# Five unread products per chunk in the gather loop of a graph-network kernel

## The chip, the cores and the metric

The kernel runs on one core of a Trainium2 chip. The metric is the device time of one execution in microseconds (us), as the median of several runs. The core has a tensor engine (PE), whose weight loads are listed apart as PEld, a vector engine (DVE), a scalar engine (ACT), GpSimd (POOL), a sync engine (SP) that issues transfers, and 16 DMA engines. The profile also lists the granted clock of the tensor engine as a share of full speed.

## The reference

The program is eight residual stages over a graph with 6250 nodes of 256 features and 100000 edges (`src`, `dst`): four graph layers and four mixtures of experts, in turn. Stage 3 is the second graph layer:

```python
def _L1_gnn_ref(vertex_features, edge_index, w0, w1):
    w0_features = vertex_features @ w0
    w1_features = vertex_features @ w1
    dst, src = (edge_index[0], edge_index[1])
    messages = w1_features[src]
    neighbours = jax.ops.segment_sum(messages, dst, num_segments=vertex_features.shape[0])
    return jax.nn.relu(w0_features + neighbours)
...
x = x + _L1_gnn_ref(_layernorm(x, axis=-1), edge_index, L1_gnn_w0, L1_gnn_w1)
```

It is called with `edge_index = jnp.stack([src, dst])`, so what the layer calls `dst` is the graph's `src`. Each node sums the transformed features of its neighbours.

## The kernel before

The stages run one after the other in one program, all unrolled. The features stay in on-chip memory as 49 tiles of 128 nodes (`X`), and each stage adds its result there.

Stage 3 has two halves. The first normalizes each tile, multiplies it by both weights, keeps the `w0` part in the accumulator `acc3` and writes the `w1` part to the table `w1d` in DRAM. A row of that table is 768 bf16 numbers: three bf16 parts of each of the 256 f32 values, so that their sum carries the precision of f32.

The second half is the loop of the change. The edges were sorted earlier, during stage 1, into buckets of 128 target nodes, and the buckets are cut into chunks of 256 edges (two lanes of 128). There are 448 chunks (`NCH`). Each chunk does this:

- On POOL, `gather` (line 631) fetches for each of the two lanes 128 rows of `w1d` by an indirect DMA into a tile `row3`. Six such tiles take turns (`s3g`, `bufs=6`), so a gather needs the tile of six gathers before, three chunks back.
- On DVE, once for every four chunks, line 1104 builds the one-hots `sel` of the target nodes of eight lanes. Two such tiles take turns.
- On PE, line 1113 forms six products of 256 columns: for each lane the one-hot matrix is the weight, and the three parts of the rows stream through. All six add up in one PSUM tile, `nbp` in the profile, of which there are two.
- On DVE, line 1116 adds this PSUM tile to the accumulator of the bucket, whose number DVE loads into a register, eight chunks at a time (`buckets`).

Beside the loop runs the sorting of stage 4's edges. It is a generator, `bucket_move`, of which `next(steps, None)` issues one step per chunk. It first counts edges per bucket (PE line 228, DVE line 220), then places them (PE lines 303 and 305, DVE's predicated copy on line 308), then moves them group by group (DVE's one-hots on lines 340 to 345, PE line 348) and scatters them to DRAM from POOL (line 327). Its products use PSUM tiles called `small` and `mv`.

The order on each engine in this stage is that of a list scheduler: an instruction that comes earlier in the program goes first when it is ready. The engines then work through their lists in order. Semaphores between them are placed from the tiles that instructions read and write.

Of the kernel before, what the change touches and what calls it, by code (L numbers as in the profile page):

```python
# [8 lines left out]
F = mybir.dt.float32  # L9
# [39 lines left out]
class Kern:  # L49
# [1013 lines left out]
    def stage3(self, S, routes):  # L1063

        tc, nc, A, X = self.tc, self.nc, self.A, self.X
        wd = self.dram.tile([NP, 3, D], BF, name="w1d")
        with ExitStack() as big:
            bp = big.enter_context(tc.tile_pool(name="s3", bufs=1))
            acc = bp.tile([128, NT, D], F, name="acc3")
            with ExitStack() as cx:  # L1070
                mp = cx.enter_context(tc.tile_pool(name="s3st", bufs=1))
                wp = cx.enter_context(tc.tile_pool(name="s3w", bufs=3))
                pp = cx.enter_context(tc.tile_pool(name="s3p", bufs=2, space=PSUM))
                W = self.kxm(mp, "W01", [A["L1_gnn_w0"], A["L1_gnn_w1"]])
                mv, rs = self.norm_stats(mp, wp, "s3")
                for t in range(NT):
                    hT = self.norm_T(wp, pp, mv, rs, t)
                    wps = pp.tile([128, 512], F, name="wps")
                    for k in range(2):
                        nc.tensor.matmul(wps, hT[:, k, :], W[:, k, :], start=(k == 0), stop=(k == 1))  # L1080
                    nc.scalar.activation(acc[:, t, :], wps[:, :D], AF.Copy)
                    o = wp.tile([128, 3, D], BF, name="w1o")
                    r = wp.tile([128, D], F, name="w1r")
                    self.parts([o[:, j] for j in range(3)], r, wps[:, D:])
                    nc.sync.dma_start(wd[t * 128:(t + 1) * 128], o)
            wdf = wd.rearrange("n j d -> n (j d)")
            with ExitStack() as cx:
                kp = cx.enter_context(tc.tile_pool(name="s3k", bufs=1))
                gp = cx.enter_context(tc.tile_pool(name="s3g", bufs=6))
                sp = cx.enter_context(tc.tile_pool(name="s3s", bufs=2))  # L1090
                pp = cx.enter_context(tc.tile_pool(name="s3q", bufs=2, space=PSUM))
                NCH, G = S["NCH"], 4
                iog = kp.tile([128, 128, 2 * G], BF, name="iog")
                nc.vector.tensor_copy(iog, self.iotab.unsqueeze(2).to_broadcast([128, 128, 2 * G]))
                locb = kp.tile([128, 2 * NCH], BF, name="locb3")
                nc.vector.tensor_copy(locb, S["sl"][:, :, 1])
                steps = routes(cx)
                for c in range(NCH):
                    next(steps, None)
                    b = self.buckets(S, c)  # L1100
                    if c % G == 0:
                        n = 2 * min(G, NCH - c)
                        sel = sp.tile([128, 128, 2 * G], BF, name="sel")
                        nc.vector.tensor_tensor(
                            sel[:, :, :n], iog[:, :, :n],
                            locb[:, 2 * c:2 * c + n].unsqueeze(1).to_broadcast([128, 128, n]),
                            ALU.is_equal)
                    ps = pp.tile([128, D], F, name="nbp")
                    for k in range(2):
                        row = gp.tile([128, 3 * D], BF, name="row3")  # L1110
                        self.gather(row, wdf, S["idx"][:, 2 * c + k, 0:1])
                        for j in range(3):
                            nc.tensor.matmul(ps, sel[:, :, 2 * (c % G) + k], row[:, j * D:(j + 1) * D],  # L1113
                                             start=(k + j == 0), stop=(k == 1 and j == 2))
                    ab = acc[:, ds(b, 1), :].rearrange("p o d -> p (o d)")
                    nc.vector.tensor_add(ab, ab, ps)
                for _ in steps:
                    pass
            for t in range(NT):
                nc.vector.scalar_tensor_tensor(X[:, t, :], acc[:, t, :], 0.0, X[:, t, :],  # L1120
                                               op0=ALU.max, op1=ALU.add)
# [1104 lines left out]
```

## Time and profile before

| what | value |
|---|---|
| median of 9 runs | 10914.83 us (10907.68 to 10940.94) |
| the profiled execution | 10896.95 us |
| its span, first to last instruction | 10895.2 us |
| instructions | 105592 |
| PE busy | 6449.9 us (59%), 32431 products |
| DVE busy | 5113.6 us (47%) |
| POOL busy | 4550.0 us (42%) |
| mean granted clock of PE | 0.729 |
| stage 3's loop | 3518.8 to 5045.0 us |

How to read it: a group of instructions is listed as line, engine, operation, the tile written and the tiles read, the number of instructions, then busy time in us and the mean of one in ns, and then the time that the engine sat idle just before them and what ended it. Products overlap in PE's pipeline, so the duration of one is longer than the distance from one start to the next. A list of waits gives who waited for whom, the us in total, the number of waits and the longest. A list of stretches gives start and end, the length, busy us and number of instructions of each engine, then the granted clock, the busy share of the DMA engines and GB/s.

### The profile page before, as it was taken

How to read it: one execution, taken by the hardware profiler on the slowest of the kernel's cores; microseconds unless marked ns; L12 is line 12 of the kernel's file. 1: busy time of each engine (PE TensorE's matmuls, PEld its weight loads, DVE VectorE, ACT ScalarE, POOL GpSimd, SP SyncE). 2: the span in 40 equal slices, each digit the busy share in tenths (PEclk: the TensorE clock that was granted, in tenths of full speed). 3: DMA queues.
4: the chain of work that ended last, by engine and by line, in shares of the span. 5: the costliest groups of instructions: out<-in, count | busy, mean ns of one | idle time of the engine just before them, and what ended most of it. 6: DMA issues, size and time to landing. Idle time of an engine off the chain costs nothing. (4 is left out here: it accounts for less than half of the span.)

```text
span 10895.2 us, 105592 instructions
## 1 busy us (share of the span) xinstructions
PE 6449.9 (59%) x32431; PEld 4201.3 (39%) x32431; DVE 5113.6 (47%) x13299; ACT 2222.3 (20%) x6799; POOL 4550.0 (42%) x4498
## 2 busy tenths in 40 slices
PE   4787657634794776665455555395555552742494
PEld 1345444422571333333233333174244442531363
DVE  5568755456314455543455555712333337333204
ACT  1243346520232000000222222131211110211120
POOL 0246655410123667673444444024266660243211
PEclk9888778765897766665566666597777775776597
DMA  3444356542662443334000000065444442452222
GB/s 130 149 137 112 108 149 195 157 119 79 193 209 92 136 125 106 104 107 91 7 7 7 7 7 7 2 214 167 115 122 117 121 114 75 153 155 47 54 78 66
DMA packets 613936, 1128.30 MB, mean 104 GB/s; under 512 B 156477, under 2 KB 420222, under 8 KB 599270
## 3 DMA queue, kind: packets, MB, share of 16 engines
q0 software_dynamic: 234752, 600.59, 21.0%
q1 hardware_dynamic: 320167, 454.29, 13.6%
q10 hardware_dynamic: 58412, 66.25, 2.0%
q8 instruction: 271, 4.44, 0.2%
q14 instruction: 334, 2.74, 0.1%
HBM read 930.96 MB, written 189.76 MB: 103 GB/s over the span
## 5 line engine op out<-in xcount | busy, mean ns | idle before, releaser
L766 PE MATMUL ops<-roww,ow 128*128 128x260 f32 (+1 forms) x3136 | 1017.5, 473 | 494.1 <-issue 288.7
L631 POOL DMA_INDIRECT roww<-kvd,saidx x784 | 845.8, 1079 | 1014.2 <-PE small L228 385.9
L631 POOL DMA_INDIRECT row<-gatd,scsl x864 | 817.0, 946 | 826.7 <-DVE pv L1684 542.3
L631 POOL DMA_INDIRECT row<-w1d,sbsl x896 | 901.7, 1006 | 551.9 <-issue 176.2
L631 POOL DMA_INDIRECT roww<-zd,saidx x784 | 813.5, 1038 | 581.8 <-issue 220.9
L766 PEld LDWEIGHTS ops<-roww,ow 128*128 128x128 f32 x3136 | 706.2, 239 | 702.4 <-issue 327.7
L1113 PE MATMUL nbp<-row,sel 128*128 128x256 bf16 x2688 | 566.0, 358 | 367.3 <-DMA row<-w1d,sbsl 216.2
L754 ACT ACTIVATE roww<-roww,pw 128x64 f32<-128x64 f32 x3136 | 756.9, 333 | 11.3 <-issue 9.2
L348 PE MATMUL mv<-orr,ol 128*128 128x234 f16 (+1 forms) x1824 | 545.3, 444 | 213.4 <-DVE orr L345 167.7
L1113 PEld LDWEIGHTS <-sel 128*128 128x128 bf16 x2688 | 366.0, 155 | 615.5 <-issue 335.3
L1030 PE MATMUL qe<-qw,ohT 128*128 128x256 bf16 x2352 | 419.4, 317 | 298.8 <-DVE roww L1033 229.8
L1649 DVE TENSOR_REDUCE mg<-P 128x4 f32<-128x1024 f32 x432 | 526.7, 1219 | 124.6 <-PE P L1644 83.1
L1352 PE MATMUL yp<-wr,hr 128*128 128x256 f32 x2176 | 537.9, 387 | 51.1 <-DVE yr L1355 50.8
L1390 PE MATMUL hp<-xr,wr 128*128 128x256 f32 x2176 | 535.8, 398 | 28.6 <-ACT hr L1392 19.0
L1355 DVE TENSOR_TENSOR yr<-yp,br 128x256 f32<-128x256 f32 x328 | 138.9, 424 | 861.7 <-PE yp L1352 806.6
L1149 PE MATMUL tps<-ident,xn 128*128 128x128 f32 x490 | 124.8, 404 | 686.0 <-DVE xn L126 470.1
L1641 PE MATMUL P<-identb,mb 128*128 128x512 bf16 x864 | 477.3, 552 | 11.9 <-issue 11.9
L1644 PE MATMUL P<-rb,sel 96*128 96x512 bf16 x864 | 466.2, 540 | 0.0
L1390 PEld LDWEIGHTS hp<-xr,wr 128*128 128x128 f32 x2176 | 401.7, 196 | 144.9 <-ACT hr L1392 29.2
L1033 DVE TENSOR_TENSOR roww<-roww,qe 128x512 f32<-128x512 f32 x448 | 270.6, 613 | 381.6 <-DMA roww<-kvd,saidx 199.1
L1352 PEld LDWEIGHTS yp<-wr,hr 128*128 128x128 f32 x2176 | 408.1, 194 | 106.8 <-DVE yr L1355 55.8
L1030 PEld LDWEIGHTS <-ohT 128*128 128x128 bf16 x2352 | 251.5, 112 | 442.9 <-issue 270.3
(629 smaller groups left out, 12520.5 us busy)
## 6 DMA issues: line engine op xcount, KB each, us to landing
wr<-in_moe_dram SPq DMA_DIRECT2D x108, 1026.0 KB
lr<-salaned SPq DMA_DIRECT2D x112, 448.0 KB
yd<-yr SPq DMA_DIRECT2D x164, 256.0 KB
wr<-in_moe_dram SPq DMA_DIRECT2D x56, 513.0 KB
eat<-in_edge_attr_dram ACTq DMA_DIRECT2D x32, 781.2 KB
qw<-qd SPq DMA_DIRECT2D x112, 192.0 KB
br<-in_L_ffn_b_dram SPq DMA_DIRECT2D x164, 128.0 KB
main<-osb SPq DMA_DIRECT2D x112, 129.0 KB
```

The lines of the kernel that those rows point to most:

```text
L348: nc.tensor.matmul(mv, ol[:, :, i], orr[:, 0:2, :, i], start=(c + i == c0), stop=(c + i == c0 + n - 1))
L631: return self.nc.gpsimd.indirect_dma_start(out=out, out_offset=None, in_=table, in_offset=bass.IndirectOffsetOnAxis(ap=idx, axis=0))
L754: nc.scalar.activation(x, x, AF.Copy, scale=p[:, j, i * H + h:i * H + h + 1])
L766: nc.tensor.matmul(ps[:, :VW], ow[:, j, :], row[:, j, v0:v0 + VW], start=(j == 0), stop=(j == BW - 1))
L1030: nc.tensor.matmul(ps[:, b], ohT[:, j + b, :], qw[:, k], start=(k == 0), stop=(k == 2))
L1033: nc.vector.tensor_mul(kr, kr, ps[:, :m])
L1113: nc.tensor.matmul(ps, sel[:, :, 2 * (c % G) + k], row[:, j * D:(j + 1) * D], start=(k + j == 0), stop=(k == 1 and j == 2))
L1352: nc.tensor.matmul(yp, hT[:, k, i * 128:(i + 1) * 128], w[:, O2 + k * D:O2 + (k + 1) * D], start=(k == 0), stop=(k == KH - 1))
L1390: nc.tensor.matmul(hp, w[:, k * H + m * 128:k * H + (m + 1) * 128], xe[:, k], start=(k == 0), stop=(k == 1))
L1641: nc.tensor.matmul(P[:, k], st["mb"][:, :, 2 * i + k], self.identb.unsqueeze(1).to_broadcast([128, 4, 128]), start=True, stop=False)
L1644: nc.tensor.matmul(P[:, k], sel[:, 2 * i + k, :], st["rb"], start=False, stop=True)
L1649: nc.vector.tensor_reduce(st["mg"][:, i, :], st["P%d" % i].rearrange("p k h e -> p h k e"), AX.XY, ALU.max)
```

## The change

Behind the six products of a chunk, five more are issued. Each multiplies the one-hots of the chunk's second lane with the first 512 columns of the second lane's row tile, and writes a PSUM tile `spare3` of 512 f32 columns, of which there is one. Each starts a sum of its own and ends it, and nothing reads the tile.

```diff
                 steps = routes(cx)
+                spare = pp.tile([128, 512], F, name="spare3", bufs=1)
                 for c in range(NCH):
...
                         for j in range(3):
                             nc.tensor.matmul(ps, sel[:, :, 2 * (c % G) + k], row[:, j * D:(j + 1) * D],
                                              start=(k + j == 0), stop=(k == 1 and j == 2))
+
+                    for _ in range(5):
+                        nc.tensor.matmul(spare, sel[:, :, 2 * (c % G) + 1], row[:, 0:512], start=True,
+                                         stop=True)
                     ab = acc[:, ds(b, 1), :].rearrange("p o d -> p (o d)")
                     nc.vector.tensor_add(ab, ab, ps)
```

## The prediction

> **What bounds the kernel now.** I read the page first, then the busy time of the engines in three parts of stage 3's loop, then the waits inside the loop, then TensorE's timeline, and last the loop in stretches of 20 us.
>
> The page says where the loop lies and who is busy in it: 448 chunks, 6 products each (2688) on line 1113, two gathers each (896) on line 631.
>
> ```profile
> L631 POOL DMA_INDIRECT row<-w1d,sbsl x896 | 901.7, 1006 | 551.9 <-issue 176.2
> L1113 PE MATMUL nbp<-row,sel 128*128 128x256 bf16 x2688 | 566.0, 358 | 367.3 <-DMA row<-w1d,sbsl 216.2
> ```
>
> The loop runs from the first gather at 3518.8 us to the last add at 5045.0, 1526 us. It has three parts: the first 480 us, in which other work counts and places stage 4's edges (512-column products of lines 228, 303, 305); 800 us of line 348's products with scatters; and a tail of 246 us with the loop alone. Busy time of PE, its granted clock, then DMA share and GB/s:
>
> ```profile
> 3520.00:4000.00 480.00, 357.69 (x1434) 0.72 0.49 138
> 4000.00:4800.00 800.00, 553.03 (x2290) 0.69 0.38 105
> 4800.00:5046.00 246.00, 119.34 (x463) 0.51 0.58 121
> ```
>
> PE is busy 1030 of 1526 us. POOL is the pacer: 896 gathers and 144 scatters are busy 1056 us, and 0.30 us of issue lies before each (1040 x 0.30 = 312), together 1368. The 158 us left are real waits; most name PE, since a gather has to wait until PE is done with the row of six gathers before:
>
> ```profile
> PE nbp L1113 <- DMA row<-w1d,sbsl: 216.2, 222, 10.2
> POOL row L631 <- PE nbp L1113: 140.9, 206, 4.6
> ```
>
> So the loop sits between two engines: PE waits for rows, and POOL for PE to free them. What PE is given more can lie in its 496 idle us, or come out as late rows.
>
> **What one added product costs.** Before has no product of these operands with 512 columns; the nearest are stage 4's bf16 products of 512, back to back (start, duration):
>
> ```profile
> 5399.90 0.63 PE L1644 MATMUL P<-rb,sel 96*128 96x512 bf16 x1
> 5400.33 0.63 PE L1641 MATMUL P<-identb,mb 128*128 128x512 bf16 x1
> ...
> 5404.13 0.38 PE L1641 MATMUL P<-identb,mb 128*128 128x512 bf16 x1
> 5404.35 0.38 PE L1644 MATMUL P<-rb,sel 96*128 96x512 bf16 x1
> ```
>
> The granted clock was 0.50 around the first pair and 1.00 around the second. From start to start that is 0.43 us at 0.50 and 0.22 at 1.00, so five cost 2.15 or 1.10 us per chunk, and 448 chunks 963 or 493 us of PE. The durations, 0.63 and 0.38, overlap and would be too much. The five weight loads are hidden behind 0.22: line 1113's load has a median of 0.147 us, and ten products of 256 columns took 1.31 us at 3705.87, 0.13 each, so the load keeps that pace. Without that cover five would cost 5 x 0.15 = 0.75 more.
>
> **Which clock.** The stretches around these lines show both:
>
> ```profile
> 3680.00:3700.00 20.00, 18.58 (x59) 0.50 0.48 131
> 3700.00:3720.00 20.00, 15.08 (x72) 0.91 0.50 135
> 4000.00:4020.00 20.00, 18.98 (x82) 0.95 0.49 139
> 4060.00:4080.00 20.00, 8.03 (x27) 0.50 0.29 79
> ```
>
> Idle stretches are at 0.50, most fully busy ones near 0.9. In the tail the six products take 1.44 us a chunk at 0.50 and would be 0.84 at 1.00 (the six at 4300.31). With the five, PE has more to do in every stretch, so I take 0.83 inside the loop: five cost 1.10 / 0.83 = 1.32 us. The clock may also not rise: at 3687.57 to 3699.90 PE was busy 12.16 of 12.33 us, still at 0.50.
>
> [...]
>
> **The sum.** Nothing is removed or moved. Added are 2240 products and their loads on PE and one PSUM tile; no DMA, no DVE or POOL instruction. Nobody reads the tile, so it makes no consumer wait. Behind the five in PE's queue stand the next products of the other work (lines 228, 303, 305, 348) and the next chunk's six. For those wait: DVE's add (line 1116), its predicated copy (308) and its one-hots (340), and POOL, because the chunk's second row is now free only after the five. DVE's add should not wait for the five, as its sum is complete before them; if it did, 448 x 1.32 = 591 us would be the most it could cost.
>
> I lay the five over 77 stretches of 20 us: busy PE time of the stretch, plus its chunks (products of line 1113 divided by 6) x 1.32, minus 20, where positive. At 4000 us: 18.98 + 6.33 x 1.32 - 20 = 7.3 us too much; at 4060: 8.03 + 2 x 1.32 = 10.7, nothing. The overflow is 99 us in the first part, 104 in the second and 3 in the tail, 206 in all. If the own six are first brought to 0.84 us a chunk, because the clock is higher, it is 119. Stretches of 40 us, in which more evens out, give 176 and 91. The mean of the four is 148; I take 150 us. 20 us is the nearer size: six row buffers hold three chunks, about 10 us. At 1.10 the four lie between 44 and 139, at 2.15 between 341 and 524.
>
> The same from the buffers: a row's buffer comes round once in three chunks, so a delay of 1.32 costs at most 1.32 / 3 = 0.44 us a chunk, 197 us in all; nothing where a row waits for POOL anyway. In the tail POOL needs 2 x 1.25 = 2.5 us a chunk and PE 0.84 + 1.10 = 1.94, and a chunk takes about 3.2 us today: the five are hidden there behind the gathers. If that cover were gone, the tail would pay 76 x 1.10 = 84.
>
> Two small terms are bounded. The order in which the other work's products stand among the chunks may shift a little: between a gain and a loss of 50 us (a third of the 158 us of POOL's waits), taken as zero. The instruction stream grows by 4480 of 105592, 4.2%; the queue that brings it is busy 0.2% of 16 engines, so I take zero, and 20 us at the most.
>
> The profiled execution took 10896.95 us (span 10895.2 and 1.75 around it), 18 us below the median of the nine runs, 10914.83. With 150 us it would take 11047; the median then is 11065. What measurement can tell from no change is about 0.2%, 22 us.
>
> **The rivals.** *Hidden.* PE's 496 idle us hold the 493 that five cost at full clock, and POOL goes on pacing: 10893 to 10937. For it: the tail, and the stretches of scatters, in which PE is idle half the time. Against it: the stretches that are 15 to 19 of 20 us full. A form of it is that products nobody reads are not issued at all; then the profile would show none. Chance 0.13.
>
> *Faster.* The denser queue holds the clock up, the own six shrink from 1.44 to 0.84 us a chunk, and rows come free sooner. POOL's waits that name PE are 181 us over 269 waits, less 269 x 0.30 of issue, so 100 us is all there is: 10815 at best, 10865 at half. It decides where the 0.60 saved on the six counts and the 1.10 behind them falls into PE's wait for the next row; but the second row of each chunk is released after the five. Chance 0.06.
>
> *Cold.* The clock stays near 0.50 as at 3687 us, five cost 2.15, and the overflow is 341 to 524: 11255 to 11440. It decides if DVE's hold-ups of PE (up to 8 us in the waits) drop the clock in each group of the second part and the work between does not lift it. Chance 0.16.
>
> **How the numbers follow.** The forecast, 11065, is an overflow of some 25 to 340 us; it has 0.65. Its own range is 10940 to 11255. The range that should hold 8 in 10 is 10915 to 11320: below it lie the gain and half of the hidden case (0.06 + 0.065), above it a part of the cold one. Faster by over 0.2%: 0.06; within 0.2%: 0.13; slower: 0.65 + 0.16 = 0.81.
>
> **What would show it.** Right: 2240 products of 128x512 on the new line, starting 0.22 to 0.43 us apart; the loop some 150 us longer, nearly all before the tail; a granted clock of about 0.8 in the first two parts and above 0.51 in the tail; fewer us of PE waiting for rows, more of POOL waiting for PE with the new line as the name; stages before and after as long as now. Wrong: a tail that grows by more than 25 us (the five are not hidden there), a clock near 0.6 (cold), or POOL's waits for PE unchanged (hidden, or the cost is elsewhere).

## The result and the profile after

The kernel with the five products takes 10972.97 us (median of 10 runs, 10962.11 to 10993.07). The kernel before, run beside it again, takes 10920.66 us (31 runs), so the ratio is 1.0048, with a 95% interval from 1.0039 to 1.0057: 52 us slower. The forecast was 150 us. The sign and the range were right; the size was not, at about a third of the forecast.

From the page of the kernel after, the groups that answer to those shown of before. The loop's lines have moved: the six products stand on line 1114, the five on 1118, DVE's add on 1121.

```profile
L631 POOL DMA_INDIRECT row<-w1d,sbsl x896 | 907.7, 1013 | 600.8 <-issue 168.0
L1118 PE MATMUL spare<-row,sel 128*128 128x512 bf16 x2240 | 591.1, 395 | 3.0 <-issue 2.3
L1114 PE MATMUL nbp<-row,sel 128*128 128x256 bf16 x2688 | 424.0, 287 | 157.0 <-DMA row<-w1d,sbsl 141.7
```

All 2240 products are there. Against before, the six lost a quarter of their busy time (566.0 to 424.0 us), and the mean of one fell from 358 to 287 ns. That is the clock: from start to start they take 0.213 us at a granted clock of 0.50 and 0.109 at 1.00.

For the comparison by parts I cut the loop at events and not at fixed times: from the first gather to line 348's first product in the loop, to its last product, and to the last add. Busy time of PE and its granted clock, before:

```profile
3518.80:3971.80 453.00, 332.56 (x1332) 0.72 0.49 139
3971.80:4796.40 824.60, 576.02 (x2384) 0.69 0.39 105
4796.40:5045.00 248.60, 121.48 (x472) 0.51 0.57 120
```

and after:

```profile
3530.90:3988.50 457.60, 406.70 (x2093) 0.98 0.49 137
3988.50:4853.80 865.30, 750.89 (x3459) 0.91 0.37 100
4853.80:5107.90 254.10, 168.26 (x876) 0.93 0.59 121
```

The loop grew from 1526 to 1577 us, and 41 of these 51 us lie in the second part. The first part and the tail, which got about half of the products, pay 5 us each. The clock went to 0.98, 0.91 and 0.93. Outside the loop DVE, ACT and POOL run the same instructions in the same order; the loop starts 12 us later and what follows it takes 5 us less, and both are taken as variation between executions. Inside the loop the order on PE, DVE and POOL is not that of before, since the scheduler made it anew with the five in it.

The waits inside the loop, after:

```profile
POOL row L631 <- PE nbp L1114: 165.8, 210, 3.3
PE nbp L1114 <- DMA row<-w1d,sbsl: 141.7, 126, 10.9
POOL row L631 <- PE spare L1118: 65.0, 76, 2.6
```

PE waits less for rows (216.2 to 141.7 us), and POOL waits more for PE: 140.9 before, and now 165.8 for the six and 65.0 for the five. This fits a row that is held too long as well as a PE that is simply behind. The experiments had to tell these apart.

### The profile page after: what moved, and what is told of

It reads as the page before. It is cut to its first block, busy times and chain, and to the rows that moved or that the text cites. A ratio compares the mean times of both kernels' runs of the same rounds, so it can differ in the third digit from the quotient of the medians.

```text
span 10952.9 us, 110097 instructions
## 1 busy us (share of the span) xinstructions
PE 6763.9 (62%) x34671; PEld 4463.1 (41%) x34671; DVE 5117.2 (47%) x13299; ACT 2223.9 (20%) x6799; POOL 4546.7 (42%) x4498
## 5 line engine op out<-in xcount | busy, mean ns | idle before, releaser
L1118 PE MATMUL spare<-row,sel 128*128 128x512 bf16 x2240 | 591.1, 395 | 3.0 <-issue 2.3
L1114 PE MATMUL nbp<-row,sel 128*128 128x256 bf16 x2688 | 424.0, 287 | 157.0 <-DMA row<-w1d,sbsl 141.7
L1114 PEld LDWEIGHTS <-sel 128*128 128x128 bf16 x2688 | 324.6, 147 | 340.8 <-issue 285.4
```

The source lines that it names most:

```text
L1118: nc.tensor.matmul(spare, sel[:, :, 2 * (c % G) + 1], row[:, 0:512], start=True, stop=True)
```

## The experiments

The runs were made on several chips, on which the kernel before takes between 9909.5 and 11002.5 us, so each is compared with the kernel before on its own chip. Differences in us are the ratio, less 1, times that median. The parts of the loop are named first, second and tail as above.

Four causes were tried against each other. **A**: PE's time; the higher clock repays the five except where PE is full at that clock as well. **B**: the second row of each chunk is freed only after the five. **C**: the new list order of the loop. **D**: DVE's one-hots wait for line 348's products, which stand behind the five.

**Five products that hold no row**

```diff
+                fixw = kp.tile([128, 128], BF, name="fixw3")
+                fixr = kp.tile([128, 512], BF, name="fixr3")
+                nc.vector.tensor_copy(fixw, acc[:, 2, 0:128])
+                nc.vector.tensor_copy(fixr, acc[:, 0:2, :].rearrange("p o d -> p (o d)"))
...
-                    for _ in range(5):
-                        nc.tensor.matmul(spare, sel[:, :, 2 * (c % G) + 1], row[:, 0:512], start=True,
-                                         stop=True)
+                    with tc.issue_after(six.ins):
+                        for _ in range(5):
+                            nc.tensor.matmul(spare, fixw, fixr, start=True, stop=True)
```

Here `six` is the last of the chunk's six products, and `issue_after` keeps the five behind it.

> The five products stay behind the six, but read two tiles filled once before the loop, so they hold no row and no one-hots (two DVE copies are added). Theory A (the cost is PE's time in the stretches that were full already): as with the change, +35 to +65 us against before. Rival B (the cost is the row that is freed only after the five): 0 to +15 us.

Measured: 1.0055 (1.0034 to 1.0077), +55 us. The cost is all there without any hold on a row, so B falls: it allowed 15 us at the most, and the interval begins at 34.

**Two products, and ten**

```diff
-                    for _ in range(5):
+                    for _ in range(2):
```

> Two products in place of five, 0.44 us a chunk at full clock. Theory A (PE's time, repaid by a clock that rises): the clock in the loop is 0.8 to 0.9, and the time -15 to +15 us. Rival B (held rows): in proportion, about +20. Rival C (the list order of the loop, which the scheduler made anew, costs): +40 to +60 whatever the number of products.

Measured: 1.0023 (1.0001 to 1.0044), +23 us. With ten (`range(10)`):

> Ten products in place of five, 2.20 us a chunk at full clock. Theory A: PE is full in the first two parts; a chunk needs 0.84 + 0.65 + 2.20 = 3.7 us in the first and 0.84 + 1.50 + 2.20 = 4.5 in the second, so the first part grows by 120 to 180 us, the second by 110 to 190 beyond the change, the tail by at most 30: +280 to +420 us against before. Rival B (held rows, in proportion): about +100. Rival C (order): about +50.

Measured: 1.0411 (1.0380 to 1.0442), +408 us, at the upper end of what A gave. The three parts with ten:

```profile
3356.80:3921.30 564.50, 553.56 (x2790) 0.99 0.39 111
3921.30:4942.80 1021.50, 966.22 (x4475) 0.97 0.31 85
4942.80:5195.20 252.40, 229.12 (x1235) 0.97 0.59 121
```

PE is now busy 98% of the first part and 95% of the second. On a chip with nearly the same time of the kernel before (9909.5 us there, 9934.7 here) the kernel before takes 408.5, 778.6 and 232.2 us for the three parts. So two, five (the run above, without a hold on a row: 412.1, 824.2, 237.5) and ten cost about 4, 4 and 156 us in the first part, and about 22, 46 and 243 in the second. The first part takes five almost free of charge and then fills up; the second pays from the start, and steeply once it is full. Two cost a little more than A expected, and they lifted the clock to 0.93, 0.82 and 0.70 in the three parts without a gain anywhere. C expected +40 to +60 at any number, which +23 does not fit well (the interval, +1 to +44, just reaches it) and +408 does not fit at all; B's proportion fails at ten, too.

**The five on one side of the loop alone**

```diff
-                    for _ in range(5):
+                    for _ in range(5 if 150 <= c < 372 else 0):
```

> The five products only for the 222 chunks 150 to 371, those beside line 348's products. Theory A (PE is full there, and line 348's products gain nothing from the clock): nearly the whole cost of the change, +30 to +50 us. Rival B or a cost spread evenly over the chunks: half of it, +20 to +30.

Measured: 1.0050 (1.0034 to 1.0066), +50 us: half of the products, the whole cost. The other half:

```diff
-                    for _ in range(5):
+                    for _ in range(0 if 150 <= c < 372 else 5):
```

> The five products only for the 226 chunks 0 to 149 and 372 to 447, those without line 348's products. Theory A: the clock repays them there, 0 to +12 us against before, with a clock above 0.9 in the first part and the tail. Rival (a cost spread evenly over the chunks): +20 to +30.

Measured: 1.0009 (0.9993 to 1.0026), +9 us, not told from zero. On this run's chip one more profile of the kernel before was taken.

> The kernel before once more, for a profile on the same chip as the next three. Both theories: its time is that of the kernel before beside it, and the three parts of its loop are the yardstick for the others.

It took 9906.85 us, beside a median of 9909.5. Its three parts, and below them those with the five outside the second part:

```profile
3356.70:3765.20 408.50, 315.60 (x1332) 0.78 0.54 154
3765.20:4543.80 778.60, 581.10 (x2383) 0.68 0.40 111
4543.80:4776.00 232.20, 124.38 (x474) 0.52 0.61 130
```

```profile
3357.80:3772.60 414.80, 395.98 (x2082) 0.98 0.54 152
3772.60:4551.00 778.40, 577.69 (x2382) 0.68 0.40 111
4551.00:4786.20 235.20, 159.36 (x852) 0.95 0.63 129
```

The added products of the first part are 750, those of 150 chunks, and come to 150 x 1.08 = 162 us of PE (0.216 us from start to start). Its busy time grew by 80, and the part by 6. The higher clock, 0.98 in place of 0.78, gave back the rest.

**More buffers**

Eight row tiles in place of six, without and with the five:

```diff
-                gp = cx.enter_context(tc.tile_pool(name="s3g", bufs=6))
+                gp = cx.enter_context(tc.tile_pool(name="s3g", bufs=8))
```

> No added products; eight row tiles in place of six. It is the yardstick for the next run. Both theories: POOL waits less for rows, -10 to -80 us.

> The five products, with eight row tiles. Theory A (PE and POOL both need nearly all their time beside line 348's products, and six rows are too few to even out their order): the products still cost, but less than with six, +10 to +40 us against the eight-row kernel without them. Rival (PE is simply full in the second part, so no buffer helps): +40 to +60 against it.

Measured: 0.9989 (0.9973 to 1.0005) without the five and 1.0035 (1.0023 to 1.0047) with them. Between the medians, 9903.67 and 9949.8, lie 46 us, so the five cost about what they cost with six. That lies in the range of the rival named there, that PE is simply full and no buffer helps, and not in mine; but the two intervals together leave some 20 us either way, so the pair does not fully part them. Whether eight rows alone are a gain is not settled.

Three buffers for what DVE prepares for line 348's products, without and with the five:

```diff
-                ol = wp.tile([128, 128, BT], H16, name="ol")
+                ol = wp.tile([128, 128, BT], H16, name="ol", bufs=3 if nm == "sc" else 2)
...
-                orr = wp.tile([128, 3, W, BT], H16, name="orr")
+                orr = wp.tile([128, 3, W, BT], H16, name="orr", bufs=3 if nm == "sc" else 2)
```

> No added products; three in place of two buffers for the one-hots of line 340 and the operand of lines 342 to 345, in stage 3's loop alone. It is the yardstick for the next run. Both theories: -15 to +5 us.

> Three buffers, with the five products. Theory A (PE is full): the five still cost +30 to +55 us against three buffers without them. Rival D (DVE waits for buffers behind the five): the third buffer takes the wait away, 0 to +20.

Measured: 0.9999 (0.9983 to 1.0014) and 1.0039 (1.0022 to 1.0056), a difference of 0.40% or 44 us, some 25 us either way (the medians, 10993.29 and 11049.15, lie 56 apart). DVE does wait longer for line 348's products when the five are there: its line 340 waited 63.8 us for them before and 113.1 after. With three buffers it is 1.5 us without the five and 78.0 with them. The third buffer took away only a part of the wait, and the cost stayed. So this pair speaks against D but does not exclude it; the next section shows what DVE waits behind.

**Line 348's products made cheaper**

What is left is that PE is full in the second part. Line 348's products in the trace of before, at a granted clock of 0.50; PE, start and duration:

```profile
4556.74 2.08 PE L348 MATMUL mv<-orr,ol 128*128 128x234 f16 x6
4558.64 1.03 PE L1113 MATMUL nbp<-row,sel 128*128 128x256 bf16 x4
```

and in the trace after, at 1.00:

```profile
4319.98 2.06 PE L348 MATMUL mv<-orr,ol 128*128 128x234 f16 x6
4321.85 0.84 PE L1114 MATMUL nbp<-row,sel 128*128 128x256 bf16 x6
4322.53 1.24 PE L1118 MATMUL spare<-row,sel 128*128 128x512 bf16 x5
4323.61 2.04 PE L348 MATMUL mv<-orr,ol 128*128 128x234 f16 x6
```

After, one chunk takes 3.63 us of PE, from 4319.98 to 4323.61, without a gap. Line 348's six take 1.87 of them, 0.31 each, and at half the clock they took 1.90 (4556.74 to 4558.64), 0.32 each. Over the whole second part of before, the median from start to start is 0.315 us at 0.50 and 0.314 at 1.00. POOL needs 2.5 us for a chunk's two gathers (2 x (0.95 + 0.30)). Without the five PE would need 2.55, so they turn an even race into one that PE loses by 1.1 us a chunk.

It is lost in some stretches only. PE's and then the scatters' busy time in three stretches of the kernel after:

```profile
4120.00:4140.00 20.00, 20.00 (x97) 1.00 0.48 129
4140.00:4160.00 20.00, 20.00 (x105) 1.00 0.44 118
4180.00:4200.00 20.00, 16.65 (x63) 0.76 0.24 64
```

```profile
4120.00:4140.00 20.00, 0.00 (x0) 1.00 0.48 129
4140.00:4160.00 20.00, 0.00 (x0) 1.00 0.44 118
4180.00:4200.00 20.00, 8.31 (x8) 0.76 0.24 64
```

Where POOL has scatters, each costs it about 1.3 us more (8.31 / 8 and 0.30 of issue) and PE has room for the five; where it has none, PE is full. The same holds over the whole second part, cut into spans from the first product of one chunk to that of the next. In the spans in which no scatter runs, PE was busy 311 of 387 us before (131 spans) and 466 of 472 after (149 spans). In those with a scatter it was 263 of 438 us before and 284 of 392 after. So where the five cost time, PE has no idle time in which it could be waiting for DVE; the longer waits of theory D fit as a consequence of the full PE and not as a cause of their own.

To test this, line 348's products were to take less of PE. The first attempt changed the layout, so that the columns that stream through PE lie side by side:

```diff
-                orr = wp.tile([128, 3, W, BT], H16, name="orr")
+                if nm == "sc":
+                    orb = wp.tile([128, BT, 3, W], H16, name="orr")
+                    orr = orb.rearrange("p b j w -> p j w b")
+                else:
+                    orr = wp.tile([128, 3, W, BT], H16, name="orr")
```

> No added products; the operand that streams through line 348's products is stored so that its 234 columns lie side by side, and DVE writes it with a stride instead. It is the yardstick for the next run. Both theories: the products start 0.10 to 0.16 us apart in place of 0.31 at full clock; DVE's lines 342 and 345 get slower by an unknown amount, so the time may be anywhere from -40 to +150 us.

> The same layout with the five products. Theory A (in the second part PE is full because line 348's products keep 0.31 us at any clock): the five now fit, and cost 0 to +15 us against the same layout without them. Rival D (the one-hots on DVE wait for line 348's products, which stand behind the five): the cost stays, +25 to +50.

Measured: 1.1097 (1.1075 to 1.1119) without the five and 1.1052 (1.1029 to 1.1076) with them. Both lie outside what was expected: +1207 us without the five, and 50 us less with them than without. DVE's instructions on these tiles went from 0.52 to 3.4 us each, so DVE set the pace, and the pair says nothing on A. It shows something else. The second part was 2031 us without the five and 1956 with them, with DVE busy for 1829 and 1833 us and the granted clock at 0.52 and 0.64 (one profile each): the five were a gain here. Without them DVE waited longer for PE to finish with a buffer; DVE's waits in the second part, without and with:

```profile
DVE ol L340 <- PE mv L352: 112.0, 13, 16.2
```

```profile
DVE ol L340 <- PE mv L352: 23.1, 7, 4.7
```

The second attempt keeps DVE's layout and takes four columns at a time in place of six, as stage 1 does:

```diff
-    K.stage3(K.made["sb"], lambda cx: K.bucket_move(cx, K.keep, "sc", ei[1], ei[0], E1, clamp=N - 1))
+    K.stage3(K.made["sb"], lambda cx: K.bucket_move(cx, K.keep, "sc", ei[1], ei[0], E1, clamp=N - 1, BT=4))
```

> No added products; the one-hots and operands of lines 340 to 348 are built for four columns at a time in stage 3, as in stage 1, in place of six. In stage 1 line 348's products start 0.21 us apart, in stage 3 0.31; with four they should start 0.21 apart here too, 107 us of PE less in the second part. There are more steps (about 460 in place of 370), so the last ones run behind the loop. It is the yardstick for the next run. Both theories: -20 to +60 us.

> Four columns at a time, with the five products. Theory A (the second part pays because line 348's products keep PE full whatever the clock): a step needs 4 x 0.21 in place of 6 x 0.31 us, so the five fit, and cost 0 to +20 us against four columns without them. Rival E (something else in the second part charges for each chunk's five, such as POOL's scatters behind the longer queue): +35 to +55.

Measured: 1.0021 (1.0009 to 1.0033) without the five, 1.0021 (1.0006 to 1.0036) with them, both against the kernel before. The medians are 10949.36 and 10947.77 us: the five cost nothing that can be told from zero, and the two intervals leave some 20 us either way. Line 348's products now start 0.21 us apart. PE, with the five:

```profile
4301.23 0.84 PE L1114 MATMUL nbp<-row,sel 128*128 128x256 bf16 x6
4301.91 1.24 PE L1118 MATMUL spare<-row,sel 128*128 128x512 bf16 x5
4303.47 1.00 PE L348 MATMUL mv<-orr,ol 128*128 128x234 f16 x4 [0.32 <-issue]
4304.29 0.84 PE L1114 MATMUL nbp<-row,sel 128*128 128x256 bf16 x6
...
4307.88 0.49 PE L1114 MATMUL nbp<-row,sel 128*128 128x256 bf16 x3 [0.51 <-DMA row<-w1d,sbsl]
```

A chunk needs 0.68 + 1.08 + 0.82 = 2.6 us of PE (five products of 0.216 make the 1.08), about what POOL needs, and PE waits for rows again. From the start of line 348's products to the loop's end, without the five and then with them:

```profile
3984.00:5027.30 1043.30, 611.53 (x2788) 0.62 0.42 111
```

```profile
4005.20:5048.10 1042.90, 811.05 (x4272) 0.91 0.43 112
```

PE is busy 200 us more, in the same time. Both halves of the edit help A: a step has four products in place of six, and each is cheaper. It also spreads the steps over the rest of the loop, so this run does not say how much of the relief each brings.

## Why the prediction was right and wrong

**Right.** The sign, the bound (POOL paces, PE has room, and the room decides), and that nearly all of it lies before the tail, which was to stay within 25 us and grew by 5. The price of one product was right, too: 0.216 us from start to start at full clock, and the 0.22 taken from stage 4. The weight loads were hidden: the five's have a median of 0.143 us, and the products start 0.216 apart. DVE's add does not wait for the five: in 263 of the 448 chunks it starts before the last of its chunk's five has ended. The longer instruction stream left no mark outside the loop: what follows the loop took 5 us less.

**Wrong.** The step that failed is the clock: "With the five, PE has more to do in every stretch, so I take 0.83 inside the loop: five cost 1.10 / 0.83 = 1.32 us". It was 0.98, 0.91 and 0.93, and all but 7% of the added products ran at a granted clock of 1.00. With 1.10 us in place of 1.32 the mean of the four sums falls from 148 to 89. The second half of the same error is that two of these four left the six products at the old clock. With the six at full clock too, the sum over 20 us stretches gives 66 us (21, 45 and 0 in the three parts) and that over 40 us gives 44. Measured are 5, 41 and 5.

That 66 is near to the measured 52 is partly luck. The 0.84 us for the six is a duration, of which some 0.16 overlap the next product (they take 0.68 from start to start, 4321.85 to 4322.53 above). With 0.68 the two sums would be about 38 and 17, so the sum doesn't hold all of the cost. The forecast also laid about half of its main sum into the first part (99 of 206 us), which paid 5.

What the runs showed in its place: the clock repays the added work, and it repays unevenly. In the first part the other work's products follow the clock as well (line 305's start 0.40 us apart at 0.50 and 0.23 at 1.00), and the sum had left them at their time of before, so there even the 21 us were too many. In the second part line 348's products keep 0.31 us at 0.50 and at 1.00, and that part pays. The sum came near to the cost there because it left all other work as it was, which by luck is right for these products; the trace of before shows that they do not follow the clock, and the prediction made no use of it.

One row misled me: PE 12.16 of 12.33 us busy at a clock of 0.50. I made of it that a busy PE may stay cold. After the change the longest stretches of the second part at 0.50 (20.5 us from 4388.3, 13.7 from 4289.3) are those with scatters, in which PE was busy 59% and 42%. Why the clock stayed at 0.50 in that row, no run shows. For the loop as a whole the price at full clock was the better choice: with the five at 1.10 us the sum was 44 to 139 us, and 52 was measured.

**The rivals.** *Hidden* holds for half of the products (+9 us, from -7 to +26) and, within some 20 us, for all of them once line 348's products are cheaper. *Cold* did not occur. *Faster* did not occur in this kernel: no part of the loop got shorter with the higher clock. It did where DVE paces and waits for PE to free its two buffers, in the layout run (2031 to 1956 us in the second part, at a clock of 0.52 and 0.64).

Open is why two products already cost about 22 us in the second part, almost half of what five cost. The parts there were compared across two chips, and the interval of that run (1.0001 to 1.0044) is too wide to settle it. In the spans without a scatter PE was already busy 341 of 376 us in that run, which fits A but does not prove it. A run that keeps the new list order and takes the products' time away was not made, so C is only disfavoured: by two products at +23 us, by ten at +408, and by the five at no cost with four columns. The prediction took the order as unchanged but for small shifts, at nothing with 50 us either way; the order in the loop did change, and what that alone costs is not shown.

## What to carry to other kernels

Price added tensor work at the clock that it will itself bring about (here 0.98, 0.91 and 0.93 in place of 0.72, 0.69 and 0.51 in the three parts), and apply that clock to all the work beside it; then ask which products do not follow the clock (here line 348's, 0.315 us at 0.50 and 0.314 at 1.00), because there nothing is repaid. Lay the added time over short stretches, part by part, since the idle time of a part is of no use where the engine is already full. Ask also which engine would gain by a higher clock: here POOL paced, and a clock of 0.93 in place of 0.67 over the loop gained nothing (1526 to 1577 us); in the layout run, where DVE paced and waited for PE, the time with the five was 50 us less.

## What the runs showed of the hardware

Line 348's products keep a pace that goes with how their streamed operand lies in memory, and at two of three layouts the clock does not change it. These are medians from start to start. 234 columns of two bytes, 12 bytes apart, take 0.315 us at a clock of 0.50 and 0.314 at 1.00 (before). 8 bytes apart they take 0.211 us at 0.50 and 0.210 at 1.00 (four columns, without the five). Both come to about 8.9 bytes of the operand's extent per ns (234 x 12 / 314 and 234 x 8 / 210). Side by side they take 0.194 us at 0.50 and 0.100 at 1.00 (the layout run with the five), and there they follow the clock. The weights, `ol`, still lay 12 bytes apart in that run (and in the kernel before a load of them took 0.13 us), so it is the streamed operand that set the pace and not the weight load. At full clock the columns 8 bytes apart take twice the time of those side by side, 0.210 against 0.100.

The five also lifted the granted clock of the loop's first part from 0.72 to 0.98, and its time changed by 5 us. In the layout run DVE lost by writing with a stride: 702 elements of two bytes took 0.52 us before and 3.35 there, on the line that only writes the strided tile.
